# Reordering a two-layer gated cross-attention kernel: nested branches, moved norms and additions, shared score banks, paired result rows

## The chip, the cores and the metric

The kernel is one program on one core of a Trainium2 chip. The metric is the device time of one launch in microseconds (us), the median of several runs. In the text PE is the matrix engine (PEld is its weight load, which overlaps it), DVE the vector engine, ACT the scalar engine with the activation functions, POOL the general engine, and SP the queue that issues most DMA transfers. Each engine carries out its own list of instructions strictly in the order in which it was written; engines wait for each other through semaphores. Each float32 product stands in the trace as two PE records (72 products `gu` of 36 tiles are 144 records).

## The reference: what is computed

The input x has 16 sequences of 128 tokens with 256 features, and there is a context of the same shape. Four stages follow each other, each as `x = x + tanh(g) * stage(layernorm(x))`:

- **stage 1**, an mLSTM attention with 8 heads: `q` is the normed x, `k` and `v` are the context; two gate projections of `[q, k, v]`, a cumulative sum of the forget gate, a running maximum, `D = exp(log_D - max)`, `h = (qk * D / normalizer) @ v`, and a layer norm of h with a scale;
- **stage 2**, a mixture of 8 experts with hidden size 512, two of them chosen per token, and 2 shared experts that see every token: `silu(x @ w1.T) * (x @ w3.T) @ w2.T`;
- **stage 3**, an attention with 16 heads of 16 features over the context, with a mask, and softmax;
- **stage 4**, a mixture of 16 experts with hidden size 64 in 4 groups, of which two groups and then four experts are chosen per token, and a shared expert with hidden size 512.

Because the experts differ per token, the tokens of stage 2 and stage 4 are sorted by expert (stage 4: by group) into tiles of 128 slots; each tile is gathered by an indirect DMA, computed, and its 128 result rows are scattered by an indirect DMA into a table in DRAM (`y0_d`, and `y1_d` for each half of the sequences). Each token has two such rows, which are read back and added.

## The kernel before

**Order of the work.** The order is written out by hand. `at(step, place, *fs)` puts functions into a list, `run(b, place)` issues them; the loops over steps b issue the fixed parts of a step between three places 0, 1 and 2. Inside `manual_schedule` each engine gets its instructions in just this order. Sequences come in 4 groups of 4 (g = 0 to 3), and step b of stage 1 and of stage 3 works on sequence b.

**Stage 1 (lines 857 to 891).** A step b issues: the loads `load_v` and `mlstm_load` (the row maxima of b+2, spread over all partitions, tile `dm`), `value_copy` (POOL), `mlstm_scores(b, 0)` (PE `qp`, then the DVE products `ct` with `dm`), place 0, `mlstm_scores(b, 1)`, `mlstm_values(b-1)` (PE `hp`, ACT copy `hs`), `mlstm_decay(b+1, 0)` (POOL masks `dm` at L474, ACT takes exponents at L481), `mlstm_close(b-2)` (the norm's end and the addition to x), place 1, `mlstm_back(b-1)`, `mlstm_decay(b+1, 1)`, place 2. `mlstm_back` turns `hs` back on PE (`pb`, L519), runs seven DVE operations from the normalizer `nrm` to the norm's moments `hmv` (L522 to L532), and two on POOL for the root `hrs` (L534, L535). `qp0` and `qp1` are one PSUM bank each, so the next `qp` waits until DVE has read the last one.

Around a group's first step come `ln_stats` / `ln_apply` / `ln_turn` (moments, normed rows, PE transposes `ln_tp` with an ACT copy), `gate_proj` (PE `gps`: for each of two gates two blocks from the normed x and two from the context), `gate_act`, `gate_scan` (the DVE scans that end in `gmx`) and `mlstm_rows` (PE `mps`, which spreads `gmx` for the first two sequences). `small_loads` holds four small operations of which one is an ACT Tanh; it stands at step -2, place 0, ahead of `k_proj`, whose ACT copies need `bkm` from it. `shared_scale(e)` multiplies a 128x1024 weight tile by a gate on POOL (L582), at steps 4 and 5, place 0. The shared experts' `gp`, `up` and `yp` products fill PE from step 6 on.

**Sort 0 and stage 2.** `route0` sorts the tokens; `slot_tokens` turns the summed products into the tokens `ti` to gather and the rows `di` to scatter to. 35 tiles are always run; `tiles(35, 36)` and `tiles(36, 39)` stand in two branches one after the other (L972, L974), of which this input takes neither. A branch that is not taken still makes every engine with work in it add to its semaphores. Then the last group's shared expert runs (L986 to L1000), with the addition of the first four sequences' rows, their moments, the norm and its transposes.

**Stage 3.** A step issues `scores(b)` (PE `sp0` to `sp3`, one PSUM bank each), `values(b-2)`, and then twice: `turn` of two blocks of exponents of the step before (PE `tp`, ACT copy `pT`), `softmax` of two blocks (DVE minimum L1103, ACT exponents L1109), and place 0 or 1; then `close(b-2)` (PE `pv`, DVE `o`) and place 2. The norms for the queries and for stage 4 hang on the places. The shared expert of stage 4 (`sgp`, `sup`), the query projection, the router `r1ps` and the sort's products `pre1` and `tok1` all use the two banks with the tag "e"; a gate product `sgp` holds its bank until DVE has read it. Functions named in `later` (the router's and the sort's steps) come last in their place.

**Stage 4.** `tile_step` runs tile after tile; the sort of the second half runs beside the first tiles. At the end (lines 1656 to 1677) the last eight sequences' rows are read (`read`), five by SP and three by ACT's queue, added (`last`) on POOL and DVE, and written out, beside the four products `shared4_down`.

Of the kernel before, what the change touches and what calls it, by code (L numbers as in the profile page):

```python
# [21 lines left out]
B = 16  # L22
# [41 lines left out]
NY = 3 * B * S  # L64
# [4 lines left out]
def flamingo_kernel(ctx: ExitStack, tc: tile.TileContext, a: dict, out: bass.AP):  # L69
# [70 lines left out]
    nc.vector.tensor_copy(tidxb, tidx)  # L140

# [138 lines left out]
    def small_loads():  # L280
        nc.scalar.activation(gt, gt, AF.Tanh)
        nc.vector.tensor_scalar(tf1h, tf1, 0.5, None, ALU.mult)
        nc.vector.tensor_tensor(
            bkm, bc(bk, [P, KC, 2]), hpar.unsqueeze(1).to_broadcast([P, KC, 2]), ALU.mult
        )
        nc.vector.tensor_scalar(lsg, lsg, tx0, None, ALU.mult)
# [73 lines left out]
    def gate_proj(g):  # L360
        ps = s2p.tile([P, 2, P], F32, tag="tp", name="gps", bufs=2)
        for j in range(2):
            for k in range(2 * KC):
                c = k % KC
                w_, src = (wg[:, j, c, :], xnT_g[1, g]) if k < KC else (wgc[:, j, c, :], cx_g[g])
                for i in range(GB):
                    nc.tensor.matmul(
                        ps[ts(i, 32), j, :], w_, src[:, c, ts(i, S)],
                        start=(k == 0), stop=(k == 2 * KC - 1), tile_position=(0, 32 * i),
                    )  # L370
        gate_g[g] = ps
# [207 lines left out]
    def shared_scale(e):  # L579

        w2 = shw[e][2].rearrange("p f d -> p (f d)")
        nc.gpsimd.tensor_scalar(w2, w2, tf0, None, ALU.mult)  # L582
# [21 lines left out]
    def slot_tokens(pool, tp, n, ti, di, key):  # L604

        tf = pool.tile([P, n], F32, name=key + "tf")
        nc.vector.tensor_scalar(tf, tp[:, 1, :], float(P), None, ALU.mult)
        nc.vector.tensor_tensor(tf, tf, tp[:, 0, :], ALU.add)
        nc.vector.tensor_copy(ti, tf)
        nc.vector.tensor_scalar(ti, ti, B * S - 1, None, ALU.bitwise_and)  # L610
        none = pool.tile([P, n], F32, name=key + "no")
        nc.vector.scalar_tensor_tensor(none, tf, 0.0, spare[:, 0:n], ALU.is_equal, ALU.mult)
        nc.vector.tensor_tensor(di, none, tf, ALU.add)
# [27 lines left out]
    def route0():  # L641
# [40 lines left out]

# [10 lines left out]
        for j, oh in enumerate((oh1, oh2)):  # L693
# [16 lines left out]
            nc.scalar.activation(hi[:, :, 0, :], hi[:, :, 1, :], AF.Copy, scale=pcol)  # L710
            nc.gpsimd.tensor_tensor(
                hi[:, :, 1, :], hi[:, :, 1, :], bc(tidxb[:, B + j * B : B + j * B + B], [P, B, NT0]), ALU.mult
# [36 lines left out]
    def by_token(y_d, b):  # L749

        return y_d[B * S : NY].rearrange("(j t p) d -> t p j d", j=2, p=P)[b]
# [45 lines left out]
    for g in range(G):  # L797
# [14 lines left out]
        at(s0 - 2, 0, (gate_act, g))  # L812
        at(s0 - 2, 1, (gate_scan, g))
# [19 lines left out]
    for e in range(NSH):  # L833
        at(1 + 2 * e, 0, (load_shared, e))
        at(4 + e, 0, (shared_scale, e))
# [5 lines left out]
    at(-2, 0, (small_loads,), kv[0][0])  # L841
    at(-2, 1, kv[0][1])
# [13 lines left out]
    with tc.manual_schedule(engines=ENG | {sync.engine}):  # L856
        for b in range(-4, last + 1):
            if 0 <= b < NB:
                if b == GB:
                    load_c(G - 1)  # L860
                if b + 2 < NB:
                    load_v(b + 2)
                if b + 2 < NB:
                    mlstm_load(b + 2)
                value_copy(b)
                mlstm_scores(b, 0)
            run(b, 0)
# [9 lines left out]
            if 0 <= b - 1 < NB:  # L877
                mlstm_back(b - 1)
# [95 lines left out]
    with tc.If(used > NA0 + 1):  # L974
        tiles(NA0 + 1, NT0)
# [4 lines left out]
    with tc.manual_schedule(engines=ENG | {sync.engine}):  # L980
# [6 lines left out]
        for f in range(HC0):  # L987
            shared_gate(g, f)
            for b in {1: (0,), 2: (1, 2), 3: (3,)}.get(f, ()):
                add0(b, yg[b])  # L990
            shared_up(g, f)
        ln_stats(("q", 0), s2)
# [65 lines left out]
    def big(name):  # L1058
        return s3p.tile([P, TG], F32, tag="e", name=name, bufs=2)

# [131 lines left out]
    def route4(g):  # L1192

        xnT = xnT_g["m", g]
        ps = big("r1ps")[:, 0 : GB * E1].rearrange("p (t e) -> p t e", t=GB)
# [77 lines left out]
    def sort4(hf):  # L1273
# [15 lines left out]
        pt = big("pre1")  # L1289
# [34 lines left out]
        for j in range(2):  # L1324
# [12 lines left out]
            if j == 0:  # L1337
# [7 lines left out]
            nc.scalar.activation(hi[:, :, 0, :], hi[:, :, 1, :], AF.Copy, scale=pcol)  # L1345
            nc.gpsimd.tensor_tensor(
                hi[:, :, 1, :], hi[:, :, 1, :], bc(tidxb[:, B + j * B : B + j * B + BH], [P, BH, NT]), ALU.mult
# [6 lines left out]
        tp = big("tok1")[:, 0 : 2 * NT].rearrange("p (k i) -> p k i", k=2)  # L1354
# [192 lines left out]

    for g in range(G):
# [3 lines left out]
        if g:  # L1552
            read, add, n = (
                ((-2, -1, 0, 1), (1, 2, 3, 4), 5),
                ((4, 5, 6, 7), (8, 9, 10, 11), 13),
# [6 lines left out]
            at(*divmod(n + 1, 3), (apply3, q, 0))  # L1562
            at(*divmod(n + 2, 3), (ln_turn, q, 0, s3p), (apply3, q, 1))
            at(*divmod(n + 3, 3), (ln_turn, q, 1, s3p))
# [5 lines left out]
        at(s0 + 6, 0, (apply3, m, 0))  # L1570
        at(s0 + 6, 1, (ln_turn, m, 0, s3p), (apply3, m, 1))
# [48 lines left out]
    with tc.manual_schedule(engines=ENG | {sync.engine}):  # L1620
        for b in range(-1, NB + 3):
# [15 lines left out]
            for hf in range(2):  # L1637
                if old is not None:
                    turn(old, 2 * hf)
                    turn(old, 2 * hf + 1)  # L1640
                for r in range(2 * hf, 2 * hf + 2):
# [14 lines left out]
    with tc.manual_schedule(engines=ENG | {sync.engine}):  # L1656
# [7 lines left out]
        for b in (0, 1, 2, 4, 5):  # L1664
# [4 lines left out]
        for b in (3, 6, 7):  # L1669
            read(NA + b, nc.scalar)  # L1670
        for b in range(3):
            last(NA + b, nc.gpsimd)
        for t in range(GB):
            shared4_down(m, t)
            last(NB - GB + t)
            if t == 1:
                last(NA + 3)
# [89 lines left out]
```

## Time and profile before

| | |
|---|---|
| median of the runs | 864.54 us (863.25 to 868.31, three runs) |
| the profiled execution | 868.1 us, of which the profile's span is 866.4 us |
| mean granted PE clock | 0.967 |
| busy, share of the span | PE 92%, PEld 66%, DVE 53%, ACT 42%, POOL 35% |
| stage 1 with sort 0 | 0 to about 280 us |
| stage 2's tiles | about 280 to 474 us, PE without a gap |
| stage 3 | about 505 to 705 us |
| stage 4's tiles, and the end | about 705 to 846 us, and to 866 us |

Three views are used. The table of waits says how long an engine stood idle in front of which instruction, and what it waited for. The timeline gives the instructions in order of time, with the idle time ahead of each in brackets. The windows give for a stretch of time the busy time of each engine and the granted clock of PE: 1.00 is full speed, and 0.50 half of it: the sixteen `r0ps` records took 1.95 us at 1.00 (from 92.25 us) and 3.58 us at 0.50 (from 146.59 us). Busy PE time is therefore not all useful time.

### The profile page before, as it was taken

The page shows a single profiled execution, that of the slowest core. Times are in us where ns is not written, and L with a number is a line of the kernel's source. Part 1 is how long each engine was busy: PE and PEld are TensorE (multiplying, and loading weights), DVE is VectorE, ACT ScalarE, POOL GpSimd, SP SyncE. Part 2 cuts the span into 40 slices and gives each one's busy share as a digit, 9 for nine tenths or more (in the row PEclk, how much of TensorE's full clock was granted, in tenths as well). Part 3 has the DMA queues.
Part 4 walks back from the last instruction along what each step waited for, and adds up shares of the span by engine and source line. Part 5 has one row for each costly group of instructions (what it writes and reads, how often), then busy time and mean ns, then how long its engine had stood idle before and what let it go on. Part 6 is the DMA issues. An engine that isn't in the chain of part 4 may idle for free. (4 is left out here: it accounts for less than half of the span.)

```text
span 866.4 us, 15100 instructions
## 1 busy us (share of the span) xinstructions
PE 797.6 (92%) x5084; PEld 574.4 (66%) x5084; DVE 455.8 (53%) x1756; ACT 362.0 (42%) x892; POOL 302.7 (35%) x381
## 2 busy tenths in 40 slices
PE   4977999999998999999998888889998989999996
PEld 2755666665655999999998445566665755555664
DVE  3576455464556222222222367768768775754644
ACT  3466466464111111111110147867676616444550
POOL 4125221221104555555542004840101043664642
PEclk9997998999999999999999998999999999999997
DMA  6695412100063766666661163641100021323514
GB/s 181 233 344 198 141 55 89 37 25 25 26 193 126 281 238 235 236 235 235 234 236 74 49 213 95 223 150 53 63 26 27 1 59 45 101 76 105 190 64 158
DMA packets 56590, 116.50 MB, mean 134 GB/s; under 512 B 8832, under 2 KB 39552, under 8 KB 51520
## 3 DMA queue, kind: packets, MB, share of 16 engines
q1 hardware_dynamic: 43264, 58.58, 20.6%
q0 software_dynamic: 11856, 55.62, 18.3%
q10 hardware_dynamic: 1392, 1.31, 0.5%
q8 instruction: 43, 0.70, 0.3%
q14 instruction: 35, 0.29, 0.1%
HBM read 91.10 MB, written 24.38 MB: 133 GB/s over the span
## 5 line engine op out<-in xcount | busy, mean ns | idle before, releaser
L761 POOL DMA_INDIRECT y_d<-ys,di x71 | 73.0, 1028 | 124.2 <-DVE ys L944 73.6
L928 ACT ACTIVATE tsg<-tgp 128x512 f32<-128x512 f32 x35 | 20.8, 597 | 161.4 <-PE tgp L923 98.2
L930 DVE TENSOR_TENSOR h<-tup,tsg 128x512 f32<-128x512 f32 x35 | 24.2, 692 | 115.8 <-PE tup L923 93.3
L1109 ACT ACTIVATE sc<-sc,mx 128x128 f32<-128x128 f32 x256 | 78.4, 394 | 2.6 <-DVE mx L1103 2.4
L1437 PE MATMUL gu<-wgu,xT 128*128 x144 | 69.8, 607 | 1.4 <-PEq L1431 0.8
L923 PEld LDWEIGHTS tgp<-xT,w13t 128*128 128x128 f32 x560 | 67.9, 192 | 2.4 <-DVE xT L913 0.6
L923 PE MATMUL tgp<-xT,w13t 128*128 128x128 f32 x560 | 68.3, 275 | 0.4 <-DVE xT L913 0.4
L923 PE MATMUL tup<-xT,w13t 128*128 128x128 f32 x560 | 68.2, 275 | 0.0
L940 PE MATMUL typ<-w2e,h 128*128 x280 | 66.2, 380 | 0.0
L923 PEld LDWEIGHTS tup<-xT,w13t 128*128 128x128 f32 x560 | 65.3, 192 | 0.0
L552 PE MATMUL gp<-xnT,w 128*128 128x512 f32 x112 | 57.3, 637 | 4.7 <-PEq L974 4.7
L1103 DVE CUSTOM_DVE_ANT_0 sc<-sp,mb 128x128 f32<-128x128 f32 x256 | 56.3, 286 | 8.3 <-PE sp L1090 8.3
L940 PEld LDWEIGHTS typ<-w2e,h 128*128 128x128 f32 x280 | 50.5, 190 | 5.7 <-issue 0.3
L563 PE MATMUL up<-xnT,w 128*128 128x512 f32 x112 | 53.2, 598 | 0.0
L567 DVE TENSOR_TENSOR hT<-up,sg 128x512 f32<-128x512 f32 x28 | 19.4, 692 | 61.8 <-PE up L563 40.5
L573 PE MATMUL yp<-w,hT 128*128 128x256 f32 x224 | 50.7, 381 | 0.0
L1149 POOL TENSOR_TENSOR x<-x,o 128x256 f32<-128x256 f32 x16 | 11.6, 726 | 102.4 <-DVE o L1147 98.8
L573 PEld LDWEIGHTS yp<-w,hT 128*128 128x128 f32 x224 | 41.8, 190 | 7.7 <-issue 2.3
L534 POOL TENSOR_SCALAR hrs<-hmv 128x1 f32<-128x1 f32 x16 | 3.8, 238 | 123.2 <-DVE hmv L532 123.2
L1401 POOL DMA_INDIRECT xt<-xr_d,ti x36 | 38.5, 1068 | 15.9 <-PE yp L1466 6.5
L1446 DVE TENSOR_TENSOR h<-gu,th 128x256 f32<-128x256 f32 x36 | 15.2, 424 | 52.6 <-ACT th L1444 47.5
L632 POOL DMA_INDIRECT w13t<-in_L_ffn_w_dram,wi x35 | 36.8, 1051 | 16.5 <-PE tgp L923 5.5
(316 smaller groups left out, 1633.1 us busy)
## 6 DMA issues: line engine op xcount, KB each, us to landing
yg<-y_d SPq DMA_DIRECT2D x29, 256.0 KB
dm<-m_d SPq DMA_DIRECT2D x14, 512.0 KB
kz_d<-kst SPq DMA_DIRECT2D x8, 512.0 KB
va_d<-vs SPq DMA_DIRECT2D x8, 512.0 KB
w2e<-in_L_ffn_w_T_dram SPq DMA_DIRECT2D x8, 512.0 KB
kz<-kz_d SPq DMA_DIRECT2D x4, 1024.0 KB
va<-va_d SPq DMA_DIRECT2D x8, 512.0 KB
w<-in_L_ffn_sw_T_dram SPq DMA_DIRECT2D x6, 512.0 KB
```

The lines of the kernel that those rows point to most:

```text
L552: nc.tensor.matmul(gp, shw[e][0][:, c, ts(f_, P)], xnT_g[2, g][:, c, :], start=(c == 0), stop=(c == KC - 1))
L563: nc.tensor.matmul(up, shw[e][1][:, c, ts(f_, P)], xnT_g[2, g][:, c, :], start=(c == 0), stop=(c == KC - 1))
L573: nc.tensor.matmul(yp, sh_g[g, e * HC0 + f][:, ts(t, P)], shw[e][2][:, f, :], start=(f == 0), stop=(f == HC0 - 1))
L632: nc.gpsimd.indirect_dma_start(out=t.rearrange("p j c f -> p (j c f)"), out_offset=None, in_=a["L0_ffn_w13"][:, :], in_offset=bass.Indirec ...
L761: ins = nc.gpsimd.indirect_dma_start(out=y_d[:, :], out_offset=bass.IndirectOffsetOnAxis(ap=idx[:, i : i + 1], axis=0), in_=ys, in_offset= ...
L923: nc.tensor.matmul(ps[:, f, :], wt[:, j, c, ts(f, P)], xT[:, c, :], start=(c == 0), stop=(c == KC - 1))
L930: nc.vector.tensor_tensor(h, gu[1], sg, ALU.mult)
L940: nc.tensor.matmul(yp, h[:, f, :], w2e[:, bass.ds(ev + f * D, D)], start=(f == 0), stop=(f == HC0 - 1))
L1103: nc.vector.tensor_tensor_reduce(out=sc[:, k, :], in0=sp[:, k // 2, k % 2, :], in1=masks[g][:, i, :], scale=1.0, scalar=3.0e38, op0=ALU.ad ...
L1109: nc.scalar.activation(sc[:, k, :], sc[:, k, :], AF.Exp, scale=-1.0, bias=mx[:, n : n + 1])
L1401: nc.gpsimd.indirect_dma_start(out=xt, out_offset=None, in_=xr_d[hf][:, :], in_offset=bass.IndirectOffsetOnAxis(ap=ti_h[hf][:, i : i + 1], ...
L1437: nc.tensor.matmul(gu, xT[:, c, :], wgu[:, bass.ds(ev + c * NGRP * 2 * GW, 2 * GW)], start=(c == 0), stop=(c == KC - 1),)
```

## The change

Nine edits, none of which changes what is computed:

1. `gate_proj` multiplies the context's two blocks before those of the normed x.
2. `small_loads` moves behind the second `k_proj`, to place 1 of step -2; its `bkm` becomes a function `bias_rows` that stays at place 0.
3. `shared_scale` works on a quarter (128x256) at a time, in four places one after another.
4. `mlstm_back(b-1)` at the end of step b becomes `mlstm_back(b-2)` early in step b, behind `mlstm_scores(b, 0)`.
5. The second branch of stage 2's tiles stands inside the first.
6. In the last shared expert of stage 2 the moments `ln_stats` come ahead of the last `shared_up`.
7. In stage 3 a new place, TURN, lies in the second half of a step, behind the two turns and ahead of the softmax; both `apply3` now stand at place 0, the first `ln_turn` at TURN and the second at place 2. The moments of group 2 come one place later.
8. The router's products of groups 0 to 2 and the first sort's `pre1` and `tok1` use the bank of `sp0` in place of "e".
9. A token's two result rows lie side by side in the table (row 4096 + 2 * token + j), so that reading them back is one run of 2 KB per token in place of two runs of 1 KB. At the end all eight reads are issued by SP, and the additions stand in another order on DVE and POOL.

```diff
-NY = 3 * B * S
+NY = 4 * B * S
+    twob = cst.tile([P, B], BF16, name="twob")
+    nc.vector.tensor_scalar(twob, tidx[:, B : 2 * B], 2.0, None, ALU.mult)
+    pcol2 = []
+    for j in range(2):
+        t = cst.tile([P, 1], F32, name=f"pcol2{j}")
+        nc.vector.tensor_scalar(t, pcol, 2.0, float(j), ALU.mult, ALU.add)
+        pcol2.append(t)
...
+    def bias_rows():
         nc.vector.tensor_tensor(
             bkm, bc(bk, [P, KC, 2]), hpar.unsqueeze(1).to_broadcast([P, KC, 2]), ALU.mult
         )
...
-                w_, src = (wg[:, j, c, :], xnT_g[1, g]) if k < KC else (wgc[:, j, c, :], cx_g[g])
+                w_, src = (wgc[:, j, c, :], cx_g[g]) if k < KC else (wg[:, j, c, :], xnT_g[1, g])
...
-    def shared_scale(e):
-        w2 = shw[e][2].rearrange("p f d -> p (f d)")
+    def shared_scale(e, f):
+        w2 = shw[e][2][:, f, :]
...
-        nc.vector.tensor_scalar(ti, ti, B * S - 1, None, ALU.bitwise_and)
+        nc.vector.tensor_scalar(ti, ti, 1, B * S - 1, ALU.logical_shift_right, ALU.bitwise_and)
...
-        return y_d[B * S : NY].rearrange("(j t p) d -> t p j d", j=2, p=P)[b]
+        return y_d[2 * B * S : NY].rearrange("(t p j) d -> t p j d", j=2, p=P)[b]
...
-        at(4 + e, 0, (shared_scale, e))
+        for f in range(HC0):
+            at(*divmod(3 * (4 + 2 * e) + f, 3), (shared_scale, e, f))
...
-    at(-2, 0, (small_loads,), kv[0][0])
-    at(-2, 1, kv[0][1])
+    at(-2, 0, kv[0][0])
+    at(-2, 1, kv[0][1], (small_loads,))
...
                 mlstm_scores(b, 0)
+            if 0 <= b - 2 < NB:
+                mlstm_back(b - 2)
             run(b, 0)
...
             run(b, 1)
-            if 0 <= b - 1 < NB:
-                mlstm_back(b - 1)
...
     with tc.If(used > NA0):
         tiles(NA0, NA0 + 1)
-    with tc.If(used > NA0 + 1):
-        tiles(NA0 + 1, NT0)
+        with tc.If(used > NA0 + 1):
+            tiles(NA0 + 1, NT0)
...
+            if f == HC0 - 1:
+                ln_stats(("q", 0), s2)
             shared_up(g, f)
-        ln_stats(("q", 0), s2)
...
+    def small(name):
+        return s3p.tile([P, TG], F32, tag="sp0", name=name)
...
-        ps = big("r1ps")[:, 0 : GB * E1].rearrange("p (t e) -> p t e", t=GB)
+        ps = (small if g < G - 1 else big)("r1ps")[:, 0 : GB * E1].rearrange("p (t e) -> p t e", t=GB)
...
-        pt = big("pre1")
+        pt = (big if hf else small)("pre1")
...
-        tp = big("tok1")[:, 0 : 2 * NT].rearrange("p (k i) -> p k i", k=2)
+        tp = (big if hf else small)("tok1")[:, 0 : 2 * NT].rearrange("p (k i) -> p k i", k=2)
...
-            at(*divmod(n + 1, 3), (apply3, q, 0))
-            at(*divmod(n + 2, 3), (ln_turn, q, 0, s3p), (apply3, q, 1))
-            at(*divmod(n + 3, 3), (ln_turn, q, 1, s3p))
+            at(n // 3 + 1, 0, (apply3, q, 0), (apply3, q, 1))
+            at(n // 3 + 1, TURN, (ln_turn, q, 0, s3p))
+            at(n // 3 + 1, 2, (ln_turn, q, 1, s3p))
...
-        at(s0 + 6, 0, (apply3, m, 0))
-        at(s0 + 6, 1, (ln_turn, m, 0, s3p), (apply3, m, 1))
+        at(s0 + 6, 0, (apply3, m, 0), (apply3, m, 1))
+        at(s0 + 6, TURN, (ln_turn, m, 0, s3p))
         at(s0 + 6, 2, (ln_turn, m, 1, s3p))
...
+                if hf:
+                    run(b, TURN)
...
-        for b in (0, 1, 2, 4, 5):
+        for b in range(8):
             read(NA + b, sync)
...
-        for b in (3, 6, 7):
-            read(NA + b, nc.scalar)
-        for b in range(3):
-            last(NA + b, nc.gpsimd)
-        for t in range(GB):
+        for t, (mine, others) in enumerate((((), (8,)), ((9,), (10,)), ((11,), (13,)), ((12, 14, 15), ()))):
             shared4_down(m, t)
-            last(NB - GB + t)
-            if t == 1:
-                last(NA + 3)
+            for b in mine:
+                last(b)
+            for b in others:
+                last(b, nc.gpsimd)
```

## The prediction

> **What bounds the kernel.** I read four views, the page's slices first:
>
> ```profile
> PE 797.6 (92%) x5084; PEld 574.4 (66%) x5084; DVE 455.8 (53%) x1756; ACT 362.0 (42%) x892; POOL 302.7 (35%) x381
> ...
> PEclk9997998999999999999999998999999999999997
> ```
>
> PE is the bound nearly everywhere, so an edit is worth what it takes from PE's idle time (866.4 - 797.6 = 68.8 us), and from the slices where its clock (tenths of full speed) is low. The waits of PE name that idle time:
>
> ```profile
> PE ln_tp L348 <- DVE o L1147: 4.8, 2, 2.5
> PE gp L552 <- PEq L974: 4.7, 1, 4.7
> PE qp L493 <- DVE ct L498: 3.9, 3, 1.8
> PE pb L519 <- ACT hs L511: 3.5, 5, 0.7
> PE yps L1186 <- DVE x L1190: 3.4, 1, 3.4
> PE mps L455 <- DVE gmx L394: 3.1, 1, 3.1
> PE sup L1174 <- DVE tt L1297: 2.2, 1, 2.2
> ```
>
> The columns are total us, times, longest. All stand where an edit falls; the same view has 12.7 us in front of `ln_tp` for `xn`, 9.3 of it at the start, behind the first load. The windows show what follows such a wait (the columns after the times are PE, PEld, DVE, ACT, POOL, then the granted clock):
>
> ```profile
> 65.70:75.90 10.20, 8.89 (x98) 7.24 (x98) 5.15 (x17) 3.68 (x11) 7.52 (x8) 0.50 0.77 285
> 86.10:89.60 3.50, 3.50 (x14) 2.88 (x13) 1.57 (x5) 1.45 (x3) 1.91 (x3) 0.51 0.94 300
> 144.20:154.40 10.20, 10.20 (x43) 7.10 (x40) 1.91 (x5) 3.02 (x8) 0.00 (x0) 0.50 0.35 115
> ...
> 533.30:540.10 6.80, 5.73 (x56) 4.08 (x57) 2.63 (x20) 2.02 (x5) 5.54 (x7) 0.50 0.07 18
> 577.70:581.10 3.40, 3.32 (x28) 2.21 (x32) 2.02 (x9) 0.58 (x1) 1.90 (x3) 0.50 0.00 0
> ```
>
> One more, of 3.4 us, follows 659.6. In such a stretch a product takes twice as long, so it costs PE up to half its busy time there: 1.7 us for 3.4, 5.1 us for 10.2.
>
> **The sum, part by part,** against the profiled execution's 868.1 us (the runs: 863.25 to 868.31). "Taken" is what I put into the sum.
>
> *Head (edits 1, 2).* The timeline shows who is late:
>
> ```profile
> 17.18 0.31 ACT L379 ACTIVATE ge<-ge 128x128 f32<-128x128 f32 x1
> 17.51 1.28 ACT L281 ACT_TABLE_LOAD   x1
> ...
> 18.80 0.20 ACT L281 ACTIVATE gt<-gt 128x4 f32<-128x4 f32 x1
> 19.04 0.15 DVE L282 TENSOR_SCALAR tf1h<-gt 128x1 f32<-128x1 f32 x1 [3.13 <-ACT gt L281]
> ...
> 19.90 0.41 DVE L387 TENSOR_TENSOR_SCAN gcs<-gmn,ge 128x128 f32<-128x128 f32 x1
> ...
> 21.80 0.58 PE L455 MATMUL mps<-gmx,ident 128*128 128x128 f32 x1 [3.06 <-DVE gmx L394]
> ```
>
> The scan's input is ready at 17.5, but DVE stands behind `tf1h`, which waits for the Tanh's table load. With the Tanh moved, the scan starts some 2.3 us earlier. The context's blocks need no ACT copy; they fill what PEld waits before and inside the first gate (0.33 + 0.56), taken as 0.6. So `mps` starts 2.9 us earlier, about 0.8 behind the end of `kps` (18.74 - 0.6). The first sixteen `mps` records took 3.43 us at clock 0.57, the next sixteen 1.95: 1.5 more. The Tanh now stands ahead of nothing urgent (`lsg` is first read by `mlstm_close`). Taken 4.4; bounds 2.3 (the scan alone) and 5.0.
>
> *Early steps, 50 to 92 us (edits 1, 3, 4).* PE waits 0.69, 1.35, 0.74, 0.60, 1.77, 1.31 and 2.78 us: 9.2. `qp` is late since DVE runs the back half (`nrm` to `hmv`, 63.01 to 64.95 us) ahead of `ct`; now `ct` is ahead. The two scales (2.88 us each on POOL, L582) stand in front of the mask of `dm`; now a quarter does, 0.72. The normed rows at 85.36 stand behind the back half (83.51 to 85.44) and no longer will. But the moved back half closes a loop: exponents, `ct` (0.76), back half (2.05), `hrs` on POOL (0.9), mask (1.09), four exponents (1.27), with semaphores about 6.5 us, 7.2 with a quarter scale, against steps of 7 to 9 us here. So steps 4 and 5 gain about 1.0 and 2.0 rather than all of it. Taken 3.0, and 1.5 for the clock (the window at 86.1); bounds -3 (the loop is the step) and +9.
>
> *Steps 6 on, to 250 us (edit 4).* PE fills these. `pb` stood right behind `hp` and waited 0.69 for the copy `hs` three times; now the copy is a step old. `hp` may now wait for DVE to free the bank in the three steps where the gates hold the other one. Taken 2.0, nothing for the slow 10.2 us at 144; bounds -5 (one more such stretch) and +7 (this one gone).
>
> *Branches (edit 5).* PE's branch at L972 takes 0.24 us (from 472.0), the one at L974 3.58 (from 474.4); it starts after the first one's semaphores, which wait for the last `typ`. With one branch, the long jump starts at 472.0, beside the products still running, ends at 475.6 and, with its semaphores, lets `gp` go at about 475.9 in place of 478.42: 2.5. POOL's second counting (2.27 us at L974) goes too, which issues `yg` earlier, with nobody waiting. Bounds 0.4 (the jump still starts late) and 4.2 (clock).
>
> *Moments early (edit 6).* `ln_tp` waits 1.45 us. The moments fill DVE's 1.83 us wait before the last `hT`, which itself ends some 0.5 later. Taken 1.2; bounds 0 and 1.5.
>
> *Stage 3 (edits 7, 8).* At 530 to 534 us the second `ln_tp` waits 2.55 us: the first one's copy stands behind eight exponents (2.45 us, L1109) on ACT, and holds the bank. At TURN it stands ahead of them; DVE's softmax is 0.73 later for the second pair of rows. Taken 3.0 there (with the scores behind it) and 2.5 at 577.8. At 658.2 and 700.2 `sup` waited 2.17 and 1.70 for `pre1` and `tok1` to leave "e"; but the next `sgp` needs the bank that DVE reads only at 659.66 and 700.63, so I take 0.8 and 0.5. Clock 1.7 of the 6.3 (2.9 + 1.7 + 1.7) in the three windows. Taken 8.5; bounds 2 and 13. `sp0` is free for `pre1` only once four minima of L1103 have read it, 0.8 later; counted.
>
> *End (edit 9).* Eight reads of 256 KB came at 262 GB/s, about 8 us from 849.4, and will on one queue (issue 0.5 each); the 2 KB runs are taken at nothing, bounds -1 and +1. DVE stood from 852.0 to 856.48 in front of the rows of the first late sequence, and PE 3.45 behind it. In the new order DVE ends with `x` of the fourth product at about 857.2 and three pairs of additions (0.9 each): 859.9 in place of 863.6. Taken 3.7; bounds 0.5 and 4.5. The three new small DVE operations (0.15 each, as `tf1h`) lie in its 1.32 us wait before `xn` at 8.86: nothing, 0.5 if that cover goes.
>
> Sum: 4.4 + 4.5 + 2.0 + 2.5 + 1.2 + 8.5 + 3.7 = 26.8, so 868.1 - 26.8 = 841.3, **841 us**. From the median, 3.6 lower than the profiled execution, it would be 838; I keep the higher, since new waits are likelier overlooked than gains.
>
> On the clock: the windows above follow waits of 0.7 to 2.8 us. The Trainium skill (TensorE: Matmul & The Clock Gate, Part 1) has the clock halved only by an idle window of about 3.4 us. By that rule no removed wait but the first returns any clock, and the sum would be 22.1 or less, near 846. The trace does not agree: 0.69 us of idle at 142.9 was followed by 10.2 us at 0.50, so I keep part of it.
>
> **The rivals.**
>
> *A. DVE and ACT take PE's place.* Between 510 and 700 us DVE is busy 0.54 to 0.97 of each 10 us, and 0.94 at 650. Then stage 3 gives 3, the early steps 1, steps 6 on nothing, no clock returns: 2.9 + 1.0 + 2.5 + 1.2 + 3.0 + 3.7 = 14.3, 854 us. For it: DVE's order there hardly changes. Against: DVE itself stood 3.27 us at 537.5, waiting for PE.
>
> *B. Slower: more half-speed stretches in stage 1.* The moved `pb` transposes now follow `qp`, and in steps 6, 10 and 14 join `ln_tp` and `mt`. At 140.2 to 149 us just such a stretch of small products brought 10.2 us at 0.50. Each more costs 5.1 us, in PE-bound steps. With 26.8 gained, it takes more than five new ones in the steps from 6 on to end slower; seven give 877. Against: of 12 such steps only one had a long one before. The Trainium skill says, in the same page's Part 4, that transposes do not count as busy for the gate. By that rule B would come true where transposes bunch; the trace agrees at 140, and not at 196, where eight `ln_tp` and sixteen `qp` records one after another kept 1.00.
>
> *C. The branch does not help,* since the jump still starts after the last product: 2.1 less, 843. It lies inside the forecast's range.
>
> **How the numbers follow.** The forecast with C (830 to 850): 0.64. A (850 to 860): 0.17. Gains eaten up to within 0.5% (4.3 us, about what a measurement of this kernel can tell from no change): 0.06. B and its like beyond that: 0.13. Faster 0.81, same 0.06, slower 0.13. The low end is the sum from the median, 838, less 8 for part of its upper bounds: 830; the high end takes in A: 860.
>
> **What would show it.** `mps` near 19 us with under 1 us of idle; no `pb` wait for `hs`; the mask of `dm` no longer behind a 2.9 us scale; one gap of about 2 us in front of `gp` at the branch; no `ln_tp` waiting for `o` in stage 3; DVE not waiting for `yg` ahead of the second `yps`. The prediction is wrong if `qp` waits for `ct` longer than before in steps 2 to 6 (the loop), if `hp` waits for DVE, or if more windows of stage 1 show 0.50.

## The result, and the profile after

The changed kernel takes 856.5 us (851.30 to 857.93, seven runs) against 865.21 us (861.57 to 868.31) of the kernel before beside it: a ratio of 0.989 (95% interval 0.985 to 0.992). On another chip, in the set of runs with `e5_again`, it was 0.986 (0.983 to 0.989). It is faster, and 856.5 lies inside the range given (830 to 860 us), but in the part of it that the prediction had kept for its rival A (850 to 860); the forecast was 841 us, a gain of 24 us, and 9 to 12 us came.

The profiled executions have spans of 866.4 and 854.8 us. Cut at the same instructions in both traces (the first `hp` of sequences 0 and 6, counted from 0, the first `pre`, `gp` of the last shared expert, `qps`, `gu`, and `yps` of the last four sequences), they compare as follows; what was forecast stands beside. `hp` of sequence 0 is issued in step 1 and that of sequence 6 in step 7, so the second row holds steps 2 to 6 (the recorded expectations call the same stretch "steps 3 to 5"); it ends at 108 us in the kernel before, where the prediction's early steps ended at 92 us.

| stretch | before, us | changed, us | change | forecast |
|---|---|---|---|---|
| head, from the first `ln_tp` to `hp` of sequence 0 | 35.7 | 32.4 | -3.3 | -4.4 |
| steps 2 to 6, to `hp` of sequence 6 | 63.1 | 70.3 | **+7.1** | -4.5 |
| steps 7 on, to the first `pre` | 143.6 | 144.1 | +0.5 | -2.0 |
| sort 0 and stage 2's tiles, to `gp` behind the branches | 226.7 | 224.0 | -2.7 | -2.5 |
| last shared expert, to `qps` | 26.0 | 22.6 | -3.5 | -1.2 |
| stage 3, to the first `gu` | 206.2 | 200.4 | -5.8 | -8.5 |
| stage 4's tiles, to the last four `yps` | 138.9 | 136.4 | -2.5 | 0 |
| end | 16.8 | 15.3 | -1.5 | -3.7 |

So one stretch went far the wrong way, by 11.6 us against its forecast. The windows of the changed kernel, cut at those places for steps 2 to 6, steps 7 on, stage 3 and the end (columns as before: length, then busy time of PE, PEld, DVE, ACT and POOL, then the granted clock; the last two are the share of the time in which the DMA engines were busy, and GB/s):

```profile
41.74:112.03 70.29, 61.97 (x387) 41.70 (x385) 42.58 (x129) 36.33 (x80) 22.48 (x35) 0.78 0.62 205
112.03:256.13 144.10, 139.75 (x773) 90.51 (x771) 77.91 (x225) 68.41 (x124) 25.59 (x44) 0.95 0.21 68
502.69:703.09 200.40, 185.33 (x1479) 120.01 (x1480) 158.59 (x863) 138.38 (x371) 55.31 (x73) 1.00 0.29 98
839.48:854.80 15.32, 7.07 (x33) 5.89 (x32) 7.34 (x15) 0.00 (x0) 4.66 (x6) 0.90 0.62 206
```

The same for the kernel before:

```profile
45.06:108.18 63.12, 53.88 (x386) 36.78 (x384) 41.29 (x129) 36.13 (x80) 22.82 (x32) 0.89 0.66 227
108.18:251.76 143.58, 138.82 (x772) 90.34 (x771) 75.15 (x225) 67.98 (x124) 22.54 (x42) 0.96 0.21 68
504.47:710.69 206.22, 188.78 (x1478) 123.12 (x1479) 158.21 (x863) 137.67 (x371) 55.29 (x73) 0.97 0.28 95
849.59:866.40 16.81, 9.12 (x33) 6.89 (x32) 7.17 (x15) 0.00 (x0) 4.30 (x6) 0.74 0.58 188
```

In steps 2 to 6 PE's idle time (length less busy time) fell only from 9.2 to 8.3 us, and its busy time rose by 8.1 us for the same products, since its clock fell from 0.89 to 0.78. Counted in the clock's own records, PE was busy at half speed (below: slow busy time) for 12.3 us of the stretch before, and for 29.0 us in the changed kernel. In stage 3 it is the other way round: 2.4 us of idle time and 3.5 us of slowness went.

The waits of PE in the changed kernel (total us, times, longest) show what stands there now:

```profile
PE qp L503 <- DVE ct L508: 4.2, 2, 3.5
PE sgp L1180 <- DVE hs L1195: 3.8, 4, 1.2
PE ln_tp L358 <- ACT pT L1134: 3.2, 4, 1.0
PE ln_tp L358 <- ACT xnT L359: 2.5, 4, 1.4
PE gp L562 <- PEq L984: 2.0, 1, 2.0
...
PE ln_tp L358 <- DVE ln_xn L346: 1.6, 1, 1.6
...
PE ln_tp L358 <- DVE nrm L534: 1.3, 1, 1.3
PE mps L465 <- DVE gmx L404: 1.1, 1, 1.1
```

`ln_tp` for `o`, `pb` for `hs`, `yps` for `x` and `sup` are gone, as foreseen; but `qp` waits 3.5 us at once for `ct`, and `ln_tp` and `sgp` have new waits of about 1 to 1.6 us. Two of the signs by which the prediction wanted to be called wrong are there: `qp` waits longer than before (3.5 against 1.8 us at the longest; for a late load, as will be seen, and not for the loop), and more of stage 1 stands at 0.50. Two timelines tell the early waits. DVE, near 53 us:

```profile
50.90 0.48 DVE L553 SCALAR_TENSOR_TENSOR x<-h,hrs,x 128x256 f32<-128x256 f32 x1
54.88 0.43 DVE L335 BATCH_NORM_STATS2 ln_st<-x 128x6 f32<-128x256 f32 x1 [3.49 <-DMA x<-in_x_dram]
...
55.97 0.76 DVE L508 TENSOR_TENSOR ct<-qp,dm 128x256 f32<-128x256 f32 x2
```

and PE, near 83 us:

```profile
79.45 0.66 PE L529 MATMUL pb<-ident,hs 128*128 128x128 f32 x4
81.16 0.77 PE L358 MATMUL ln_tp<-ident,xn 128*128 128x128 f32 x4 [1.05 <-DVE xn L346]
83.25 0.82 PE L358 MATMUL ln_tp<-ident,xn 128*128 128x128 f32 x4 [1.33 <-DVE nrm L534]
84.75 0.47 PE L413 MATMUL mt<-ident,gav 128*128 128x128 f32 x1 [0.68 <-ACT xnT L359]
```

In the first, in step 3, DVE stands in front of the moments of the third group's x. SP issued that load only at 47.8 us, behind 1.5 MB of weights issued from 39.5 us on, and the DMA engines were busy throughout (from 40 to 52 us their share is 0.95 or more); `ct` is behind the moments in DVE's list, and `qp` needs the bank that `ct` reads. The same wait of DVE was there before, but small, and it grows with edit 4 alone (first the kernel before, then `e2_back_alone`, which follows below):

```profile
56.63 0.43 DVE L325 BATCH_NORM_STATS2 ln_st<-x 128x6 f32<-128x256 f32 x1 [0.35 <-DMA x<-in_x_dram]
```

```profile
55.19 0.43 DVE L325 BATCH_NORM_STATS2 ln_st<-x 128x6 f32<-128x256 f32 x1 [2.58 <-DMA x<-in_x_dram]
```

In the second timeline, in step 6, `pb` lies in one of the two PSUM banks of the tag "tp" until DVE has read it (at 83.9), so the second `ln_tp` must wait for ACT's copy of the first (82.62 + 0.57 = 83.19). The profile names DVE's `nrm`, which ends at 83.22, but `ln_tp` does not read it. In the kernel before, DVE had read `pb` ahead of the norm, and the eight `ln_tp` records ran without a gap:

```profile
85.80 1.86 PE L348 MATMUL ln_tp<-ident,xn 128*128 128x128 f32 x8 [2.78 <-DVE xn L336]
```

What follows each of the two waits in the changed kernel (granted clock in the column behind POOL):

```profile
53.00:56.40 3.40, 0.00 (x0) 0.00 (x0) 1.46 (x6) 0.01 (x1) 0.00 (x0) 0.99 0.96 300
56.30:69.90 13.60, 12.62 (x88) 9.80 (x88) 12.77 (x38) 4.97 (x14) 7.53 (x11) 0.50 1.02 357
80.20:83.60 3.40, 1.11 (x7) 0.76 (x8) 3.23 (x13) 3.00 (x8) 0.50 (x2) 1.00 0.44 164
83.60:100.70 17.10, 16.42 (x60) 11.19 (x59) 3.73 (x10) 5.52 (x10) 4.95 (x7) 0.50 0.35 103
```

An empty 3.4 us is followed by 13.6 us at half speed, and 3.4 us with nothing but transposes and waits by 17.1 us. How long the half speed lasts is not fixed by these waits: in the traces of `e8_tail`, `e9_turn_old` and `e12_branch_old`, which have the same instructions and the same two waits here, the first is followed by 13.7 us again, the second by only 6.8.

### The profile page after: what moved, and what is told of

Its sections match the earlier page's. It is cut to its first block, busy times and chain, and to the rows that moved or that the text cites. A ratio compares the mean times of both kernels' runs of the same rounds, so it can differ in the third digit from the quotient of the medians.

```text
span 854.8 us, 15088 instructions
## 1 busy us (share of the span) xinstructions
PE 795.9 (93%) x5084; PEld 573.1 (67%) x5084; DVE 459.9 (54%) x1759; ACT 363.5 (43%) x892; POOL 306.5 (36%) x387
## 5 line engine op out<-in xcount | busy, mean ns | idle before, releaser
L935 PEld LDWEIGHTS tup<-xT,w13t 128*128 128x128 f32 x560 | 65.3, 192 | 0.0
L1417 POOL DMA_INDIRECT xt<-xr_d,ti x36 | 37.8, 1050 | 15.9 <-PE yp L1482 6.7
```

The source lines that it names most:

```text
L935: nc.tensor.matmul(ps[:, f, :], wt[:, j, c, ts(f, P)], xT[:, c, :], start=(c == 0), stop=(c == KC - 1))
L1417: nc.gpsimd.indirect_dma_start(out=xt, out_offset=None, in_=xr_d[hf][:, :], in_offset=bass.IndirectOffsetOnAxis(ap=ti_h[hf][:, i : i + 1], ...
```

## The experiments

**First set: is it edit 4?** `e1_no_back` is the changed kernel with edit 4 undone, `e2_back_alone` the kernel before with edit 4 alone (the lines are those of the first; the second has them the other way round):

```diff
-            if 0 <= b - 2 < NB:
-                mlstm_back(b - 2)
             run(b, 0)
...
             run(b, 1)
+            if 0 <= b - 1 < NB:
+                mlstm_back(b - 1)
```

> The changed kernel with edit 4 alone undone: `mlstm_back(b-1)` stands at the end of step b again, all else stays. Theory 1 (the early back half is what cost the time in steps 3 to 5): PE's slow busy time between the first `hp` of sequence 1 and that of sequence 6 goes from 29.0 us back to about 12 us as in the kernel before, which is worth 8.1 us of PE time, against 0.9 us of idle time that comes back: 849 us, with the 3.47 us wait of `qp` for `ct` split again into waits of 0.6 to 1.8. Theory 2 (the low clock in steps 3 to 5 comes from the other edits, or falls as it likes from run to run): within 3 us of 856.5, with 25 us or more of slow busy time in the same steps.

> The kernel before with edit 4 alone: the back half early in step b, two sequences behind. Theory 1 (the early back half costs by itself): 4 to 8 us slower than before, 869 to 873 us, with a wait of 2 us or more of `qp` for `ct` near 58 us and more than 20 us of slow busy time in steps 3 to 5. Theory 1b (it costs only together with the earlier head, since only then PE runs ahead of the load of the third group's x): within 3 us of 865. Theory 2 (edit 4 is not the cause): 861 to 865 us, waits of `pb` and `qp` gone, 3 us won.

`e1_no_back`: 848.27 us, ratio 0.986 (0.982 to 0.990); steps 2 to 6 last 63.1 us, 15.3 of it slow busy time, and DVE waits 1.25 us for the third group's x. `e2_back_alone`: 869.79 us, ratio 1.0095 (1.0065 to 1.0125), 8 us slower than before; steps 2 to 6 last 69.8 us with 20.9 us of slow busy time and more idle time (11.8 us), `qp` waiting 2.55 us near 57 and `gps` 3.8 us near 73. So edit 4 costs by itself; the stretches agree with theory 1 in both kernels. The times of `e1_no_back` do not part from the changed kernel's 0.986 to 0.989, since the slow stretches differ from execution to execution (below).

**The load and the wait.** `e3_x_first` loads the third group's x ahead of the weights; `e4_fill` fills the wait with products:

```diff
+    at(1, 0, (load_x, 2))
     for e in range(NSH):
         at(1 + 2 * e, 0, (load_shared, e))
...
-    for g in range(2, G):
+    for g in range(3, G):
         at(2 * g - 3, 2, (load_x, g))
```

```diff
+    def fill():
+        ps = s2p.tile([P, TG], F32, tag="e", name="fps", bufs=4)
+        for c in range(KC):
+            nc.tensor.matmul(
+                ps, wk[:, c, 0:P], cx_g[1][:, c, :], start=(c == 0), stop=(c == KC - 1)
+            )
+
+    at(3, 0, (fill,), (fill,))
```

> The changed kernel with one transfer moved: the third group's x is loaded at place 0 of step 1, ahead of the first shared expert's weights (1.5 MB), and not at place 2. Theory 1: the moments of that x no longer stop DVE (3.49 us in front of `ln_st`), the 3.47 us wait of `qp` falls below 1 us, the slow stretch from 56.3 us goes with it: 3 us of waiting and about 6 of clock, 847 to 851 us. Rival: the next transfer is as late (`m_d` was written at 44.4 us and SP waited until 52.3 for it, so the maxima `dm` of sequence 4 land after 57 us); the wait moves to `qp` of step 4, a whole slow stretch stays, 854 to 857 us.

> The changed kernel with two more products of 128x512 (8 records, about 3.6 us) on PE at place 0 of step 3, whose result nobody reads: they stand just where PE waits 3.47 us for `ct`. No other work is added or moved. Theory 1 (the empty 3.41 us window halves the clock for the four windows behind it): the clock stays at 1.00 from 56.3 us on, the 12.6 us of slow busy time go, and the kernel gets 5 to 6 us faster though PE has 3.6 us more to do: 850 to 852 us. Theory 3 (the low clock there comes from the small products and transposes of these steps and not from the wait): half speed at 56 to 70 us as before, 856 to 857 us.

`e3_x_first`: 849.33 us, ratio 0.987 (0.981 to 0.993); the wait of DVE is gone, steps 2 to 6 last 63.1 us with 12.5 us of slow busy time. The wait of `qp` is 2.1 us, not under 1: `ct` of the next sequence is late, behind DVE's own list, in which it worked without a gap from 48.9 to 58.7 us. Its four executions took 845.1 us at a mean clock of 0.986 and 0.983, and 855.4 and 853.5 at 0.972 and 0.974. From 0.986 to 0.972 is 24 us more at half speed (twice the difference, of 850 us) and 10.3 us more time: about 0.43 us for each.

`e4_fill`: 854.64 us, ratio 0.992 (0.990 to 0.995), not the 850 to 852 expected. In its trace the wait is filled, the clock stays at 1.00 until 62.1, and steps 2 to 6 last 65.3 us with 3.6 us more work in them; but the clock of its other executions (0.972 to 0.974) was no higher than the changed kernel's. That one empty window sets the clock of the next 13 us is not shown by it.

**Second set: how steady is it, and what else?** `e5_again` is the changed kernel once more. `e6_loads` adds to `e3_x_first` the line below; `e7_old_back_loads` is that with edit 4 undone; `e8_tail` has another order at the end.

```diff
-        at(1 + 2 * e, 0, (load_shared, e))
+        at(2 + 2 * e, 0, (load_shared, e))
```

```diff
-        for t, (mine, others) in enumerate((((), (8,)), ((9,), (10,)), ((11,), (13,)), ((12, 14, 15), ()))):
+        for t, (mine, others) in enumerate((((), (8,)), ((10,), (9,)), ((11,), ()), ((12, 13, 14, 15), ()))):
```

> The changed kernel once more, unchanged, so that the others of this set stand beside it on one chip. All theories: ratio to the kernel before near 0.989. Theory 1 says that its steps between the first `hp` of sequence 1 and that of sequence 6 last about 70.3 us again, with a wait of `qp` for `ct` of 3 us or more and more than 20 us of slow busy time; theory 2 (the clock falls as it likes) says that the stretch differs from 70.3 by more than 3 us.

> The changed kernel with the third group's x loaded at place 0 of step 1, and each shared expert's weights (1.5 MB) one step later, at steps 2 and 4. Theory 4 (steps 3 to 5 are held by the transfers: with x moved alone they lasted 63.1 us in place of 70.3, and then the maxima of sequence 4 were late, which POOL waited for): `m_d` is written without 1.5 MB ahead of it, SP waits under 3 us for it in place of 5.5, the mask of sequence 4 starts a microsecond or more earlier, the steps last 60 to 62 us, 844 to 848 us in all. Theory 5 (DVE is the bound there: in the run with x first it worked without a gap from 48.9 to 58.7 us): 62.5 to 64 us for the same steps, 848 to 851 us.

> As the run before, and edit 4 undone as well. Theory 4: 60 to 62 us for the steps, 844 to 848 us. Theory 5: DVE has the same work in another order, 62.5 to 64 us, 847 to 850 us; then edit 4 is worth nothing either way once the loads come in time, and the two kernels stand within 3 us of each other.

> The changed kernel with POOL adding sequences 8 and 9 at the end in place of 8, 10 and 13, and DVE the other six. Theory 6 (POOL's closing instruction takes 6.7 us behind its last addition and sets the end of the changed kernel: it ended at 853.98 us, 2.1 us behind the last write): DVE's last addition ends 0.9 us later, but the stretch from the first `yps` of the last four to the end falls from 15.3 us to 14.0 to 14.4. Rival (the last write sets the end): it grows by 0.9 to 16.2. The whole time moves by about 1 us, which the times cannot tell.

`e5_again`: 850.28 us, ratio 0.986; steps 2 to 6 last 69.1 us, 28.9 of it slow busy time, after a wait of only 2.2 us. With the first profile, six traces up to the next set share the changed kernel's stage 1 to the letter: 70.3, 69.1, 65.0, 64.8, 69.4 and 65.2 us, mean 67.3. With the back half at its old place and the loads as they were, four traces have 63.1, 63.1, 63.6 and 64.5, mean 63.6 (`e1_no_back`, and three with the stage 1 of the kernel before). So edit 4 costs 3.7 us there on the mean, and the 7.1 us of the profiled pair is at the upper end: three of the six are more than 3 us below 70.3, so theory 2 holds for the size of the loss, though not for its being there.

`e6_loads`: 850.22 us, ratio 0.986 (0.983 to 0.988), steps of 63.3 us: the weights' move adds nothing to the x, as theory 5 has it. `e7_old_back_loads`: 845.94 us, ratio 0.981 (0.979 to 0.983), steps of 59.6 us, near what theory 4 has. The windows of the two, `e6_loads` first:

```profile
41.30:104.58 63.28, 56.05 (x386) 37.20 (x385) 42.48 (x129) 36.24 (x80) 22.43 (x35) 0.87 0.68 226
```

```profile
40.97:100.57 59.60, 51.47 (x386) 35.08 (x385) 41.64 (x129) 36.03 (x80) 23.84 (x37) 0.94 0.72 241
```

So with the loads in time edit 4 still costs 3.7 us, with *less* idle time (7.2 against 8.1 us) and more slow busy time (15.5 against 6.8): neither theory foresaw both. The load has its effect in these steps (63.1 and 63.3 us with edit 4, where six traces with the late load have 64.8 to 70.3), but in the whole time it does not show alone (0.987 and 0.986 against the 0.986 of `e5_again`).

`e8_tail`: 851.21 us, ratio 0.987; the end lasts 13.8 us in place of 15.3 (in all, 13.8 to 14.0 in the three traces with this order, 15.3 to 15.9 in the twelve that end as the changed kernel does). The closing instruction of POOL, first in the changed kernel and then here (xcount, then shortest/median/longest in ns, then first and last start):

```profile
L1781 POOLq DRAIN  x3: 45/113/6722, 847.2 to 854.5; - x3
L1781 SPq DRAIN  x3: 7/7/7, 851.8 to 854.2; - x3
```

```profile
L1781 POOLq DRAIN  x3: 45/113/6761, 838.5 to 846.9; - x3
L1781 SPq DRAIN  x3: 7/7/7, 846.2 to 846.5; - x3
```

and in the kernel before:

```profile
L1763 POOLq DRAIN  x3: 45/113/6721, 856.8 to 866.1; - x3
L1763 SPq DRAIN  x3: 7/7/7, 865.5 to 865.8; - x3
```

The first of POOL's three takes 6.7 us. In the changed kernel it starts at 847.2, together with POOL's last addition, and ends 2.1 us after SP has seen the last write (851.8); with POOL done sooner it ends at 845.2, before SP (846.2). Theory 6 holds; as expected, the whole time does not show it.

**Third set: stage 3, the branches, and the parts together.** `e9_turn_old` and `e10_bank_old` are the changed kernel without edit 7 and without edit 8, `e12_branch_old` is it without edit 5 (each is the change's own diff, reversed); `e11_best` is `e7_old_back_loads` with the end of `e8_tail`.

> The changed kernel with edit 7 alone undone (norms and turns in stage 3 at their old places). Looked at in the stretch from the first `qps` to the first `gu`: 200.4 us in the changed kernel, 206.2 before. Theory 7 (edit 7 carries most of the gain of stage 3, partly by the clock): the waits of 2.5 and 2.2 us of `ln_tp` for `o` are back, the waits of about 1.0 to 1.6 that stand in their place go, and the stretch lasts 203 to 205 us. Rival (edit 8 carries it): 200 to 202 us.

> The changed kernel with edit 8 alone undone (router and first sort's products in the bank of the gates again). Theory 7: the waits of `sup` of 2.2 and 1.7 us are back, and the waits of `sgp` for `hs` of 1.2 and 1.0 and of `pre` of 0.7 go, so that the stretch from the first `qps` to the first `gu` lasts 200.5 to 202 us. Rival (edit 8 carries the gain): 203 us or more.

> The changed kernel with edit 5 alone undone (two branches one after another). The stretch from the first `tgp` to the first `gp` of the last shared expert lasted 195.3 us in the changed kernel and 197.9 before. Theory 8 (the forecast: the far jump starts only after the last product): PE idle 4 us or more in front of `gp`, 197.5 to 198. Theory 9 (the far jump has no fixed price: it took 3.58 us before, 3.36 in the changed kernel, and 1.69 in the run with edit 4 alone, which has the two branches one after another): idle between 2.3 and 4.7, most likely near the 2.6 of that run, so the edit is worth 0.3 to 2.6 us.

> The changed kernel with edit 4 undone, the third group's x loaded at place 0 of step 1, the shared experts' weights a step later, and POOL adding 8 and 9 at the end. If the parts add up: 845.9 us less 1.5 for the end, a ratio of 0.977 to 0.982 to the kernel before, below the changed kernel's 0.986 to 0.989; steps of 59.6 us from the first `hp` of sequence 1 to that of sequence 6. Rival (the clock takes back what the waits give): a ratio of 0.985 or more.

Stage 3 lasts 202.8 us in `e9_turn_old` (one run, 854.97 us) and 201.1 in `e10_bank_old` (one run, 856.44 us), against 200.4. So edit 7 is worth 2.4 us, a bit under what was expected, and edit 8 0.7, each read from one trace. The waits of `e9_turn_old`, and then of `e10_bank_old`, show why so little:

```profile
PE ln_tp L358 <- DVE o L1163: 4.8, 2, 2.6
PE sgp L1180 <- DVE hs L1195: 3.8, 4, 1.2
...
PE ln_tp L358 <- ACT pT L1134: 1.9, 2, 0.9
```

```profile
PE sup L1190 <- DVE tt L1313: 2.2, 1, 2.2
```

Undo edit 7 and 4.8 us of waiting for `o` come back, but 1.3 us for `pT`, 1.6 for `ln_xn` and 0.9 for `xr` go; of the 2.4 us 1.1 are idle time and 1.3 the clock. Undo edit 8 and `sup` waits 2.2 and 1.7 us again, but two waits of `sgp` (1.2, 1.0) and one of `pre` (0.7) go. What edits 7 and 8 took off is for the most part handed to DVE and ACT.

`e12_branch_old` (one run, 852.89 us) waits 2.2 us in front of `gp`, about as long as with the branches nested (2.0), and its far jump takes 1.29 us: there edit 5 is worth nothing.

```profile
PE gp L562 <- issue: 2.2, 1, 2.2
```

`e11_best`: 843.57 us, ratio 0.976 (0.973 to 0.979), with steps of 59.6 us and an end of 13.8: the parts add up, and it beats both kernels.

**Last: the bank, and the branch once more.** `e13_loads_pb_bank` is `e6_loads`, and `e17_pb_bank_alone` the changed kernel, each with

```diff
-        pb = s2p.tile([P, NH0, 2 * DH0], F32, tag="tp", name="pb", bufs=2)
+        pb = s2p.tile([P, NH0, 2 * DH0], F32, tag="e", name="pb", bufs=4)
```

`e14_before_again` is the kernel before, `e15_branch_alone` that with edit 5, `e16_best` is `e13_loads_pb_bank` with the end of `e8_tail`.

> The kernel of the run with x first and the weights a step later (edit 4 in place), and `pb` in one of the four banks of the tag "e" in place of the two that it shares with `ln_tp`, `mt`, `hp` and `gps`. With the loads in time the early back half still cost 3.7 us in steps 3 to 5 (63.3 against 59.6 us), 7.2 against 8.1 us of idle but 15.5 against 6.8 us of slow busy time. Theory 10 (`pb` holds a bank until DVE has read it, so the second `ln_tp` waits 1.33 us for the copy of the first, and a window of 3.41 us holds nothing but transposes and waiting): the waits of 1.33 and 0.68 go, slow busy time falls to 10 us or less, the steps last 60 to 61.5 us, a ratio of 0.981 to 0.984. Rival (it is DVE's order, the bank is nothing): 63 to 64 us, 0.985 or more.

> The kernel before once more, for a second look at its two branches. Theory 9 (the second jump has no fixed price): 2.1 to 2.7 us idle in front of `gp` as in the two other runs with two branches, with a jump of 1.2 to 1.8 us. Theory 8 (it is this kernel's own price): 4.5 us or more, with a jump of 3.4 us or more.

> The kernel before with edit 5 alone (the second branch inside the first). Both theories: a single jump of 3.4 to 3.8 us that starts at the first branch, 2.0 to 2.4 us idle in front of `gp`, 195.0 to 195.6 us from the first `tgp` to it. What the edit is worth is read against the run of the kernel before beside it.

> The run before (edit 4 in place, x first, weights a step later, `pb` in a bank of the tag "e") with POOL adding sequences 8 and 9 at the end. If the parts add up: a ratio of 0.969 to 0.974 to the kernel before, about 1.5 us under the run before, with 13.7 to 13.9 us from the first of the last `yps` to the end. Rival (the clock takes it): 0.975 or more.

> The changed kernel with `pb` in a bank of the tag "e" and nothing else changed; the loads are late as before. Theory 10 (load and bank are two separate causes): the wait of `qp` for `ct` stays above 2 us, the waits of 1.33 and 0.68 us near 83 us go, the steps last 64 to 66 us in place of 69 to 70, steps from the sixth sequence on 140 to 141 us in place of 144, a ratio of 0.977 to 0.983. Rival (without the load the bank is worth nothing): 69 to 70 us, 0.985 or more.

| | us | ratio to before (interval) | steps 2 to 6 | idle | slow busy | steps 7 on, idle |
|---|---|---|---|---|---|---|
| `e13_loads_pb_bank` | 839.12 | 0.973 (0.970 to 0.976) | 59.2 | 5.9 | 9.7 | 140.8, 2.7 |
| `e16_best` | 841.75 | 0.972 (0.970 to 0.975) | 59.1 | 5.9 | 9.6 | 140.8, 2.7 |
| `e17_pb_bank_alone` | 845.27 | 0.978 (0.975 to 0.981) | 61.8 | 6.4 | 15.3 | 136.5, 3.3 |

With `pb` in another bank the eight `ln_tp` records of `e17_pb_bank_alone` run in one piece again:

```profile
79.32 0.66 PE L529 MATMUL pb<-ident,hs 128*128 128x128 f32 x4
81.18 1.31 PE L358 MATMUL ln_tp<-ident,xn 128*128 128x128 f32 x8 [1.20 <-DVE xn L346]
83.18 0.33 PE L413 MATMUL mt<-ident,gav 128*128 128x128 f32 x1 [0.69 <-ACT xnT L359]
```

and its stretches of steps 2 to 6 and steps 7 on read

```profile
41.00:102.83 61.83, 55.40 (x387) 37.66 (x385) 43.07 (x129) 36.15 (x80) 22.87 (x36) 0.86 0.68 233
102.83:239.32 136.49, 133.21 (x773) 86.68 (x772) 77.33 (x225) 68.09 (x124) 25.74 (x44) 1.00 0.23 71
```

The wait of 1.33 us is gone; that of `mt`, which I expected to go too, stays at 0.7. One tag in one line is worth 0.8% (0.978 against the 0.986 of `e5_again`, each to the kernel before on its own chip, intervals apart), with the loads as late as before: the bank is a cause of its own, and the steps came out below the 64 to 66 us expected. `e13_loads_pb_bank` too was faster than expected (0.973, not 0.981 to 0.984); why is not shown. The rival, DVE's order alone, fell.

With the loads in time and `pb` in another bank, what is edit 4 worth? Steps 2 to 6 are 4.0 us under the kernel before, but most of that is the loads: `e7_old_back_loads`, with the same loads and edit 4 undone, has 59.6 us against 59.2. In these steps edit 4 takes 2.2 us of idle time (8.1 to 5.9), near the 3.0 forecast, and the clock takes 1.8 us back (51.5 to 53.3 us of busy time, 6.8 to 9.7 slow). In steps 7 on it takes the 2.0 us of idle time that were forecast (4.76 to 2.74). In the whole time `e13_loads_pb_bank` is under `e7_old_back_loads` (0.973 against 0.981, intervals apart), but `e16_best` and `e11_best`, which differ in the same way and share the new order at the end, do not part (0.970 to 0.975 and 0.973 to 0.979). The other bank with the back half at its old place was not run. `e16_best` has the lowest ratio of all, 13.97 us at the end, and does not part from `e13_loads_pb_bank` by the times.

In front of `gp` behind the branches, first `e14_before_again` (863.14 us), then `e15_branch_alone` (860.33 us, one run each):

```profile
PE gp L552 <- PEq L974: 4.5, 1, 4.5
```

```profile
PE gp L552 <- PEq L972: 2.0, 1, 2.0
```

So in the kernel before the far jump is dear again (3.35 us), and edit 5 alone is worth 2.5 us there (197.4 to 195.0 us from the first `tgp`). Theory 8 holds for that kernel; but in `e2_back_alone` and `e12_branch_old`, with two branches as well, the second jump took 1.69 and 1.29 us. What sets its price was not tried and stays open.

## Why the forecast was wrong, step by step

- **Early steps, the step that failed.** The forecast let the moved back half be held by one thing, the loop of 6.5 to 7.2 us through exponents, `ct`, back half, `hrs` and mask, and took a gain of 4.5 us. What it said of DVE's order came true (the normed rows started at 80.70 in place of 85.36). But the working followed DVE and POOL alone. For these steps it asked neither how long the moved `pb` holds its PSUM bank, which `ln_tp` needs next (it thought of the bank only for `hp`, in the later steps), nor whether the x that DVE reads ahead of `ct` has landed when DVE comes to it sooner (its wait went from 0.35 to 3.49 us). Measured: +7.1 us in the profiled pair, +3.7 on the mean of six traces against four, all of it as a lower clock; the idle time did not grow. The 1.5 us for the clock had the wrong sign, and the lower bound of -3 was too near.
- **Steps 6 on** (from step 7 in the table). Taken 2.0, measured -0.5: 0.4 us of idle time went and the clock took 0.9. With `pb` in another bank the idle time fell by the 2.0 forecast. The step failed by the same bank: in step 10 `ln_tp` now waits 1.45 and `mt` 0.68 us, in step 14 `ln_tp` 0.68.
- **Head.** 3.3 of 4.4 us, inside its bounds. `mps` starts at 19.86 with 1.1 us of idle time.
- **Branches.** 2.7 of 2.5 us, and 2.5 in the pair that changes nothing else; but not a fixed price, as said.
- **Moments.** The wait of 1.45 us is gone (1.2 forecast); the other 2 us of that stretch are the clock, and `e12_branch_old`, with edit 6 in it, lost 1.5 of them there again (24.1 us), so they are no part of the edit.
- **Stage 3.** Mis-sized: 6.8 us of waits were forecast to go and 2.4 went; the clock gave 3.5 in place of 1.7. The waits for `o` and `sup` went as described, and DVE and ACT, being next, took their place. That is rival A, as one term.
- **End.** DVE came as forecast: from the first of the last `yps` to its last addition 14.0 us before and 10.4 after, 3.6 in place of 3.7. But the sum stopped at DVE, and POOL's closing 6.7 us, hidden before (863.5, where SP closed at 865.5), became the last. That took back 2.1 us.
- **Not in the sum:** 2.5 us in stage 4. The kernel before had a slow window at 762 us in its first trace and none in its second (136.0 us there), so this is no effect of the change.

That 856.5 stands near rival A's 854 is luck: A gave the early steps a gain of 1.0 us, and they lost 7.1. Rival B named the mechanism that decided, more half-speed stretches from the moved transposes, and in step 6 also its place, where `pb` joins `ln_tp` and `mt`; the waits of step 10 brought no stretch that was not there before (10.2 us in both), those of step 14 none. It did not foresee the late x of step 3. In all, 16.7 us more of slow busy time cost 8.1 us, half of it as priced. Rival C did not come true in the profile that was forecast: the jump started at 476.3, before the last product had ended (478.1).

On the clock: the Trainium skill (TensorE: Matmul & The Clock Gate, Part 4) does not count transposes as work for the gate in the way of other products. The trace fits this at 80.2 to 83.6 us, where PE did nothing else and 17.1 us at 0.50 followed; but PE also stood idle for 2.3 of these 3.4 us, so it does not prove it. Part 1 of the same page names an idle window of about 3.4 us (the "only" is the prediction's): the empty stretch at 53.0 us is one, but in `e5_again` a wait of 2.2 us at 51.4 was followed by the same 13.7 us at 0.50. The prediction's sum by that rule keeps the clock of the first wait in its words but not in its figure: 26.8 less 1.5 and 1.7 is 23.6, not 22.1.

## What to carry to other kernels

When work is moved forward in an engine's list, follow three things: who stands behind it, how long its buffer now stays taken and who needs that buffer next, and whether everything read ahead of the critical instruction has landed at the new, earlier time. Split a stretch's change into idle time and slow time before explaining it: here the idle time fell and the time rose. Judge an edit against a kernel that differs in it alone: the gain of the steps in the best kernel came from the loads. And ask of the end which engine closes last, not only which one computes last.

## What was not expected of the hardware

- POOL's closing instruction starts with its last addition and takes 6.66 to 6.76 us in every trace of this case, and it can set the end.
- A far branch of PE took 3.35 and 3.58 us in two runs of one kernel and 1.29 and 1.69 us in two others.
- The same instruction list loses time to the clock in steps: six traces of one stage 1 fall at 64.8 to 65.2 and at 69.1 to 70.3 us, with about 18 and 29 us of slow busy time.
